# Regrouping the sparse pairs of a layer: chunks 0 to 4 and 5 to 6 instead of 0 to 3 and 4 to 6, with five buffers for fetched values

## The chip, the cores and the metric

The kernel runs on one core of one Trainium2 chip. The metric is the device time of one execution in microseconds (us); lower is better. Engines are named as in the profile: PE (TensorE, matmuls; PEld is its weight load), DVE (VectorE), ACT (ScalarE), POOL (GpSimd, which also issues the indirect gathers), SP (SyncE, which issues the plain DMAs). A "q" behind a name is that engine's instruction queue.

## The reference

Two layers, each of the form norm, modulation, mixer, gated residual, norm, modulation, experts, gated residual, on x of shape (4, 1024, 256). Cut to layer 1, which is what the change touches:

```python
B, S, H = 4, 1024, 256
h = layernorm(x) * (1 + ca) + sa
x = x + ga * fast_weights(h)              # chunks of 128 tokens, one after the other
h = layernorm(x) * (1 + cb) + sb
x = x + gb * experts(h)

def step(carry, x_chunk):                 # fast_weights: a scan over 8 chunks
    a0, a1, a2, acc = carry
    out = (silu(x_chunk @ a0) * (x_chunk @ a2)) @ a1
    loss = mean((out - x_chunk) ** 2)
    decay = 1.0 - 0.001 * loss
    return (a0 * decay, a1 * decay, a2 * decay, acc + loss), out

def experts(x):                           # E = 8 experts of 256 x 256, top 2 of them
    probs = softmax(x @ router_w.T)
    vals, idx = top_k(probs, 2)
    w = vals / (vals.sum(-1, keepdims=True) + 1e-6)
    return ((x @ W[idx] + probs[idx]) * w).sum(over the two)
```

Layer 0 has a linear attention and 8 experts with a hidden layer of 1024 and top 2; the change does not touch it.

## The kernel before

All values are float32. The token axis is cut into 8 chunks of 128 tokens; one chunk has B = 4 tiles (one for each batch) of 128 tokens by 256 features. x stays on the chip in `x_sb` during the whole kernel.

**The order of the work.** From the start of layer 1 to the end the order of the instructions on PE, ACT, DVE, POOL and SP is set by a planner, the class `Plan`. Each piece of work is given an engine, an estimated duration, the pieces it must come after, the buffers ("slots") it holds and a `rank`. `Plan.run` plays the pieces through in model time: an engine that is free takes, among the pieces that are ready and whose slots are to be had, the one of the lowest rank. The order that comes out is the order in which the instructions stand in each engine's queue, and each queue runs strictly in that order on the chip. Slots are counted in `room1`, and are freed in the order in which they were taken. Ranks count in chunks: most pieces of chunk c have ranks near c.

**Layer 1, chunk by chunk** (the loop `for c in range(NC)` at the end of the kernel):

- `combine("c1", ...)`, for each of the 4 tiles, fetches layer 0's two expert values (one plain DMA on SP into a `yg1` buffer), weighs and adds them to `x_sb`. `normal(("n1", c), ...)` norms and modulates the chunk and transposes it.
- `fast` computes the fast weights: 64 matmuls `p_u` (L1967, 128x512 outputs), the gates on ACT (L1979) and DVE (L1983), 64 matmuls `p_f` (L2015), the difference on DVE (L2037), its square on ACT (L2050), the gated step on DVE (L2056) and its addition to `x_sb` on POOL (L2063). The sum of the squares goes through the matmul `pm_loss` (L2080) to the next chunk's `decay`.
- `normal(("n2", c), ...)` norms the chunk again (`pm_t`, L1620). `routed` computes the router's logits (`pm_l`, L2107), picks two experts for each token and marks them in a group's tables. `shares` turns the logits into weights and biases. The normed rows go to DRAM (`ga_rows`, `gb_rows`; SP).

**Groups of sparse pairs.** A pair is a token with one of its two experts. Chunks 0 to 3 form group `ga` (n = 16 tiles), chunks 4 to 6 group `gb` (n = 12); the class `Pairs` holds a group's tables. When a group's last chunk has been routed, `closed` counts the pairs of each expert (`turn`, `turned`, `total`, `close`, `across`, `limits`) and ranks them (`bases`, `ranks`, `places`, `slots`). The pairs are then worked off in J = 2n + 7 blocks of 128 pairs of one expert each: 39 for `ga` and 31 for `gb`. The tables of up to 16 tiles times 8 experts fit the 128 partitions; a larger group has them in `halves`.

One block is the function `block`: `reach` on DVE (L724, once for each half), the count matmul `look` on PE (L737, once for each half), `find` on DVE (L750 and L759), a gather of 128 rows on POOL (L332, `xg`), two transposes on PE (L2259, `pm_x`), a copy on ACT (L2265), four matmuls with the expert's weights (L2276, `p_e`; two in the program, four in the trace), a copy on ACT (L2286) and a plain store to `ga_y` or `gb_y` on SP (L2289).

When all blocks of a group are stored, `combine("c2", ...)` brings the values back: for each tile two gathers on POOL (L332, `yg`) into a `yg2` buffer of which there are three, a weighing on ACT (L1504) and three steps on DVE (L1510, L1513, L1515), the last of them the addition to `x_sb`. After 4 tiles the finished chunk is stored to the output on SP (L2464).

**Chunk 7** is not sparse: `dense` multiplies it with all 8 experts (64 matmuls of 128x512, L2324) and sums with weights on DVE (L2340, L2349), then L2369 and L2370 and a store for each batch (L2373).

Ranks that matter here: blocks of `ga` run from 4.57 to 6.07 (base 4.57, span 1.5), of `gb` from 7.35 to 8.01; the combinations have 6.49 and 7.89, each plus 0.2 for each further chunk; the second norm of chunk 7 has 7.65; the dense experts have 8.23 plus 0.1 for each batch. Within a block, `reach`, the count and `find` stand 0.4 ahead of the block's own rank.

Of the kernel before, what the change touches and what calls it, by code (L numbers as in the profile page):

```python
# [19 lines left out]
P = 128  # L20
B, S, D = 4, 1024, 256
NC = S // P
KD = D // P
E = 8
# [6 lines left out]
SPARE = 3  # L31
FIRST = 8
ROUTER = 64
AHEAD = 3
DX = D + 2
W1ROW = KD * H + KH
# [102 lines left out]
def adaln_d2_kernel(  # L139
# [29 lines left out]
    ps_m = ctx.enter_context(tc.tile_pool(name="ps_m", bufs=3, space=PSUM))  # L169
# [72 lines left out]
    rank = const.tile([P, E], F32, name="rank")  # L242
# [7 lines left out]
    for dst, sign, op in ((upto16, 1, ALU.is_ge), (past16, -1, ALU.is_gt)):  # L250
# [5 lines left out]
            base=0,  # L256
# [87 lines left out]
    class Pairs:  # L344
# [4 lines left out]
        def __init__(self, pool, scratch, name, n):  # L349
            def t(shape, dt, what, of=pool):  # L350
                return of.tile(shape, dt, name=f"{name}_{what}", bufs=1)

            self.n, self.J, self.name = n, blocks_of(n), name

            self.part = min(n, P // E)
            self.halves = n // self.part
            self.K = self.part * E
            self.one = t([P, 2, n, E], F16, "one")
            self.best = t([P, 2, n], F32, "best")
            self.w = t([P, 2, n], F32, "w")  # L360
            self.pos = t([P, 2, n], F32, "pos")
            self.slot = t([P, 2, n], I32, "slot")

            self.meta = t([P, n, 2], F32, "meta")
            nc.vector.tensor_copy(self.meta[:, :, 1], twice[:, :n])
            self.beyond = t([P, 2], F32, "beyond")
            nc.vector.memset(self.beyond, float(2 * n * P))
            self.code = t([P, self.J], F32, "code")
            self.row = t([P, self.J], I32, "row")
            self.wrow = t([P, self.J], I32, "wrow")  # L370
            self.start = t([P, E], F32, "start")


            self.more = t([P, self.halves, P + 1], F16, "more")
            nc.vector.memset(self.more[:, :, P : P + 1], 1.0)
            self.limit = t([P, self.halves, self.J], F32, "limit")
            self.nth = t([P, self.J], F32, "nth")

            self.both = t([P, n + 1, E], F16, "both")
            nc.vector.memset(self.both[:, 0, :], 0.0)  # L380
            self.pairs = t([P, self.halves, P], F16, "pairs")
            self.base = t([P, self.halves], F32, "base", scratch)
# [63 lines left out]
        def turned(self, pt, h):  # L446
            nc.scalar.copy(self.pairs[: self.K, h, :], pt[:, 1, :])
            nc.scalar.copy(self.more[: self.K, h, :P], pt[:, 0, :])
# [950 lines left out]
    with tc.manual_schedule(engines=ORDERED):  # L1399
# [8 lines left out]
    ew = l1.tile([P, E, KD, D], F32, name="ew")  # L1408
    SHA, SCA, GA, SHB, SCB, GB = range(6)
    mods1 = [l1.tile([P, B, D], F32, name=f"mod{i}") for i in range(6)]  # L1410
    groups = [Pairs(l1, l1, "ga", 4 * B), Pairs(l1, l1, "gb", 3 * B)]
    mod_rows1 = dram.tile([B, 6, D], F32, name="mod_rows1")
    early = ctx.enter_context(tc.tile_pool(name="early", bufs=1))
    poolF = tc.tile_pool(name="poolF", bufs=2, side="right")
# [7 lines left out]
        p2=2,  # L1422
        pm=3,
        yg1=3,
        yg2=3,
        h1=2,
        h2=2,
        hT1=2,
# [753 lines left out]
    def closed(g, after, rank):  # L2182

        key = g.name
        ps = plan.slot("pm")

        def turn():
            made[key, "turn"] = g.turn(ps_m, 0)

        def bases():  # L2190
            made[key, "bases"] = g.bases(ps_m)

        def ranks():
            made[key, "ranks"] = g.ranks(ps_m)

        m = plan(PE, 0.3, turn, after=after, holds=[ps], rank=rank)
        t = plan(
            ACT, 0.7, lambda: g.turned(made[key, "turn"], 0), after=[m], holds=[ps], rank=rank
        )
        ps = plan.slot("pm")  # L2200
        m = plan(PE, 0.15, lambda: g.total(ps_m), after=[t], holds=[ps], rank=rank)
        d = plan(DVE, 2.3, lambda: g.close(late), after=[m], holds=[ps], rank=rank)
        ps = plan.slot("pm")
        m = plan(PE, 0.15, bases, after=[t], holds=[ps], rank=rank)
        b = plan(
            ACT, 0.2, lambda: g.based(made[key, "bases"]), after=[m], holds=[ps], rank=rank
        )
        ps = plan.slot("pm")
        m = plan(PE, 0.4, lambda: g.across(ps_m), after=[d], holds=[ps], rank=rank)
        e = plan(DVE, 0.2, g.list_experts, after=[m], holds=[ps], rank=rank)  # L2210
        d = plan(DVE, 1.1, lambda: g.limits(late), after=[e, b], holds=[ps], rank=rank)
        ps = plan.slot("pm")
        m = plan(PE, 0.3, ranks, after=[t], holds=[ps], rank=rank + 0.3)
        s = plan(
            DVE,
            0.8,
            lambda: g.places(late, made[key, "ranks"]),
            after=[m],
            holds=[ps],
            rank=rank + 0.3,  # L2220
        )
        s = plan(DVE, 0.8, lambda: g.slots(late), after=[d, s], rank=rank + 0.5)
        return d, e, s

    def block(g, j, rows, y, lists, experts, stored, rank):
# [7 lines left out]
        def count_():  # L2233
            made[key, "counts"] = g.look(ps_m, made[key, "reached"])

        hit = plan.slot("reached")
        r = plan(DVE, 0.28, reach, after=[lists], holds=[hit], rank=rank - 0.4)
        m = plan(PE, 0.15, count_, after=[r], holds=[look, hit], rank=rank - 0.4)
        f = plan(
            DVE,  # L2240
            0.6,
            lambda: g.find(late, made[key, "counts"], j),
            after=[m],
            holds=[look],
            rank=rank - 0.4,
        )
        xg, ps, xTs = plan.slot("xg"), plan.slot("pm"), plan.slot("xT")

# [47 lines left out]
    def dense(c, slotT, ts, d, x, rank):  # L2296
# [19 lines left out]
        for b in range(B):  # L2316
            last, st = [], plan.slot("step")
            for j in range(E // 2):
                ps = plan.slot("p1")

                def mm(b=b, j=j):
                    p1 = made[key, b, j] = psum(ps_1, [P, 2, D], "p1_e")
                    for k in range(KD):
                        nc.tensor.matmul(  # L2324
                            p1,
                            lhsT=made["n2", c, "hT"][:, k, b, :],
                            rhs=ew[:, 2 * j : 2 * j + 2, k, :],
                            start=(k == 0),
                            stop=(k == KD - 1),
                        )  # L2330

                def out_(b=b, j=j):
                    if j == 0:
                        made[key, "sum", b] = tiny([P, D], "step")
                    w, sum_ = made[key, "w"], made[key, "sum", b]
                    for i in range(2):
                        e = 2 * j + i
                        p = made[key, b, j][:, i, :]
                        if e == 0:
                            nc.vector.tensor_scalar(  # L2340
                                sum_,
                                p,
                                w[:, b, e : e + 1],
                                vb[:, b : b + 1],
                                ALU.mult,
                                ALU.add,
                            )
                        else:
                            nc.vector.scalar_tensor_tensor(  # L2349
                                sum_, p, w[:, b, e : e + 1], sum_, ALU.mult, ALU.add  # L2350
                            )

                m = plan(
                    PE, 1.74, mm, after=ts, holds=[ps, slotT], rank=rank + 0.1 * b + 0.02 * j
                )
                last = [
                    plan(
                        DVE,
                        0.95,
                        out_,  # L2360
                        after=[m, x, *last],
                        holds=[ps, st],
                        rank=rank + 0.1 * b + 0.02 * j - 0.5,
                    )
                ]

# [8 lines left out]
            f = plan(DVE, 0.9, done, after=last, holds=[st], rank=rank + 0.1 * b)  # L2375
            plan(SP, 0.1, store, after=[f], rank=rank)

    last_pairs = Pairs(l1, l1, "gc", B)
    lasts = {"decay": [], 0: [], 1: []}
    y_of = [dram.tile([g.J * P, D], F32, name=f"{g.name}_y") for g in groups]  # L2380
    rows_of = [dram.tile([g.n * P + 1, D], F32, name=f"{g.name}_rows") for g in groups]
    vbs = [l1.tile([P, g.n], F32, name=f"{g.name}_vb") for g in groups]
    stored = {0: [], 1: []}
    for g, rows in zip(groups, rows_of):
        for k in range(KD):
            nc.sync.dma_start(rows[g.n * P :, k * P : (k + 1) * P], ones[:1, :])
    for c in range(NC):
# [3 lines left out]
        else:  # L2391
# [16 lines left out]
        sums, decay = fast(c, slot, slotT, ts, lasts["decay"])  # L2408
        lasts["decay"] = decay
        slot, slotT, hs, ts = normal(  # L2410
            ("n2", c), c, "2", [[d] for d in sums], (SHB, SCB), 7.65 if c == NC - 1 else c + 0.92, [range(B)]
        )
        which = 0 if c < 4 else 1
        if c == NC - 1:
            d, x = routed(last_pairs, c, 0, slotT, ts, 7.46)
            dense(c, slotT, ts, d, x, 8.23)
            continue
        g, first = groups[which], 4 * which
        at = (c - first) * B
        d, x = routed(g, c, at, slotT, ts, c + 1.05)  # L2420
        shares(g, c, at, vbs[which], x, c + 1.5)
# [8 lines left out]
        stored[which].append(  # L2430
            plan(SP, 0.1, store, after=hs, holds=[slot], rank=c + 1.1, lag=3.5)
        )
        if c in (3, 6):
            lists, experts, slots = closed(g, lasts[which], c + 0.97)
            base, span = ([4.57, 1.5], [7.35, 0.66])[which]
            ys = [
                block(
                    g,
# [10 lines left out]
            for q in range(first, c + 1):  # L2449
# [7 lines left out]
                    vbs[which],  # L2457
                    mods1[GB],
                    [*ys, slots],
                    (6.49, 7.89)[which] + 0.2 * (q - first),  # L2460
                )

                def store(q=q):
# [2 lines left out]
                        x_sb[:, q, :, :],  # L2466
                    )

                plan(SP, 0.1, store, after=done, rank=(6.4, 8.2)[which] + 0.2 * (q - first))
    with tc.manual_schedule(engines=ORDERED | {EngineType.SP}):  # L2470
        plan.run()

# [56 lines left out]
```

## Time and profile before

| | |
|---|---|
| median of 3 runs | 1135.76 us (1135.41 to 1138.16) |
| profiled execution | 1146.41 us |
| its span, first to last instruction | 1144.4 us |
| mean granted TensorE clock | 0.988 |
| PE busy | 1096.9 us (96%) |
| DVE busy | 590.8 us (52%) |
| ACT busy | 425.5 us (37%) |
| POOL busy | 422.0 us (37%) |
| layer 1's first p_u matmul | at 629 us |
| group ga: last chunk's router, first fetch of a block, first gather of a combination | at 829.6, 843.4, 963.2 us |
| group gb: last chunk's router, first fetch of a block, first gather of a combination | at 1018.8, 1033.4, 1100.0 us |
| last matmul ends | at 1131.3 us |

The profile is of one execution; its time is longer than the median of the runs, and its parts are compared with its own span. A line of a group gives the line of the kernel, the engine, the operation, output and input, the number of instructions, their busy time in us and the mean duration of one in ns, and behind the second bar the idle time of the engine just ahead of them with what ended it. A line of a timeline gives the start, the length, the engine, the line and operation, and in brackets the idle time before it. A line of stretches gives the stretch, its length, the busy time and number of instructions of PE, PEld, DVE, ACT and POOL, the granted clock, the share of DMA time and GB/s.

### The profile page before, as it was taken

The numbers are of one execution on the slowest core, as the hardware profiler recorded it, in microseconds if no ns is written. First come the engines' busy times: TensorE is split into PE (matmuls) and PEld (weight loads), VectorE is DVE, ScalarE is ACT, GpSimd is POOL, SyncE is SP. The second block draws the span as 40 slices with busy tenths as digits, with TensorE's granted clock in tenths as the row PEclk, the third lists the DMA queues.
The fourth block names the chain that finished last, engine by engine and source line by source line (L and its number), as shares of the span: only waits on it lengthen the run. The fifth ranks groups of instructions, "written<-read, shape, count | busy, mean of one in ns | idle before, by whom it ended". The sixth has DMA issues, their size and how long they took to land.

```text
span 1144.4 us, 18476 instructions
## 1 busy us (share of the span) xinstructions
PE 1096.9 (96%) x6231; PEld 870.8 (76%) x6231; DVE 590.8 (52%) x2305; ACT 425.5 (37%) x1148; POOL 422.0 (37%) x483
## 2 busy tenths in 40 slices
PE   8999999999999999999999999999999999899893
PEld 5996899999999999999988466566666676656741
DVE  7777332222222222222265688866777535787566
ACT  5975233333322333332243342422425225242521
POOL 1000455555555555555553010010034332635643
PEclk8999999999999999999999999999999999999997
DMA  9424449442332415142161212100014223333543
GB/s 316 156 56 94 149 144 315 139 137 92 114 115 66 158 39 176 51 154 75 55 229 39 84 46 74 47 10 19 18 41 133 82 69 102 106 107 97 139 112 123
DMA packets 77693, 122.38 MB, mean 107 GB/s; under 512 B 27341, under 2 KB 57302, under 8 KB 72991
## 3 DMA queue, kind: packets, MB, share of 16 engines
q0 software_dynamic: 31872, 69.68, 19.7%
q1 hardware_dynamic: 44622, 49.92, 13.9%
q10 hardware_dynamic: 1104, 1.58, 0.4%
q8 instruction: 52, 0.85, 0.3%
q14 instruction: 43, 0.34, 0.1%
HBM read 205.25 MB, written 30.22 MB: 206 GB/s over the span
## 4 chain that ended last, share of the span: by engine, by line
PE 82%; DVE 7%; DMA 4%; issue 3%; ACT 2%; POOL 1%; ACTq 0%; POOLq 0%; SPq 0%; DVEq 0%
PE p_h L1658 20%; PE p_y L1681 19%; PE p_u L1967 17%; PE p_f L2015 8%; PE p_e L2276 4%; PE p_e L2324 2%; PE pm_x L2259 1%; PE pm_l L2107 1%; DMA w<-in_W,g_wrow 1%; PE pm_x L1638 1%; PE pm_counts L737 1%; PE pm_gram L1100 1%; PE pm_t L1620 1%; PE pm_b L1041 1%; PE pm_l L1233 1%
## 5 line engine op out<-in xcount | busy, mean ns | idle before, releaser
L1670 ACT ACTIVATE hid<-p_h,w 128x128 f32<-128x128 f32 x544 | 154.8, 368 | 324.7 <-issue 256.4
L1658 PEld LDWEIGHTS p_h<-xT,w 128*128 128x128 f32 x2176 | 253.1, 192 | 5.7 <-DVE xT L1643 1.6
L1658 PE MATMUL p_h<-xT,w 128*128 128x128 f32 x2176 | 254.4, 275 | 1.8 <-DVE xT L1643 1.2
L1681 PE MATMUL p_y<-w,hid 128*128 128x256 f32 x1088 | 249.0, 382 | 0.3 <-issue 0.3
L1967 PE MATMUL p_u<-hT,a 128*128 128x512 f32 x512 | 232.6, 599 | 1.7 <-ACT hf L1979 0.9
L1681 PEld LDWEIGHTS p_y<-w,hid 128*128 128x128 f32 x1088 | 201.6, 190 | 25.2 <-issue 0.5
L1967 PEld LDWEIGHTS p_u<-hT,a 128*128 128x128 f32 x512 | 94.8, 191 | 99.3 <-issue 90.4
L332 POOL DMA_INDIRECT w<-in_W,g_wrow x134 | 135.0, 1007 | 77.3 <-ACT hid L1670 47.0
L1643 DVE COPY xT<-pm_x 128x256 f32<-128x256 f32 x68 | 28.8, 424 | 186.8 <-PE pm_x L1638 143.4
L784 POOL DMA_INDIRECT y<-y,g_dest x68 | 69.5, 1022 | 143.7 <-DVE g_reached L724 108.4
L2015 PE MATMUL p_f<-a,hf 128*128 128x256 f32 x512 | 116.3, 380 | 0.8 <-ACT y L2286 0.8
L1692 DVE TENSOR_TENSOR y<-p_y,w 128x256 f32<-128x256 f32 x68 | 28.9, 425 | 167.1 <-PE p_y L1681 160.8
L332 POOL DMA_INDIRECT xg<-h_rows,g_row x68 | 66.7, 980 | 124.6 <-DVE g_hits L750 104.2
L2015 PEld LDWEIGHTS p_f<-a,hf 128*128 128x128 f32 x512 | 96.1, 190 | 18.8 <-issue 5.7
L2063 POOL TENSOR_TENSOR x_sb<-x_sb,step 128x256 f32<-128x256 f32 x32 | 24.4, 763 | 175.1 <-DVE step L2056 122.1
L332 POOL DMA_INDIRECT xg<-ga_rows,ga_row x39 | 37.3, 956 | 91.3 <-DVE ga_row L759 35.0
L2276 PE MATMUL p_e<-ew,xT 128*128 x280 | 70.4, 384 | 0.3 <-ACT y L2286 0.3
L1979 ACT ACTIVATE hf<-p_u,decay 128x512 f32<-128x512 f32 x56 | 38.2, 685 | 83.2 <-PE p_u L1967 73.6
L2276 PEld LDWEIGHTS p_e<-ew,xT 128*128 128x128 f32 x280 | 49.5, 190 | 10.3 <-issue 4.7
L1578 DVE TENSOR_TENSOR h<-h,mod 128x256 f32<-128x256 f32 x128 | 51.5, 426 | 7.0 <-ACT h L1568 3.9
L1983 DVE SCALAR_TENSOR_TENSOR hf<-p_u,decay,hf 128x512 f32<-128x512 f32 x56 | 41.9, 748 | 23.0 <-PE p_u L1967 16.3
L2286 ACT COPY y<-p_e 128x256 f32<-128x256 f32 x70 | 25.9, 371 | 56.0 <-PE p_e L2276 26.6
(362 smaller groups left out, 1291.6 us busy)
## 6 DMA issues: line engine op xcount, KB each, us to landing
yg<-y SPq DMA_DIRECT2D x32, 256.0 KB
ga_y<-y SPq DMA_DIRECT2D x39, 128.0 KB
x_sb<-in_x SPq DMA_DIRECT2D x8, 512.0 KB
h_rows<-xn SPq DMA_DIRECT2D x8, 512.0 KB
gb_y<-y SPq DMA_DIRECT2D x31, 128.0 KB
out_x<-x_sb SPq DMA_DIRECT2D x7, 512.0 KB
a<-in_fw SPq DMA_DIRECT2D x6, 512.0 KB
mod<-mod_rows SPq DMA_DIRECT2D x6, 512.0 KB
```

The lines of the kernel that those rows point to most:

```text
L332: return nc.gpsimd.indirect_dma_start(out=dst, out_offset=None, in_=table, in_offset=bass.IndirectOffsetOnAxis(ap=index, axis=0), bounds_c ...
L784: nc.gpsimd.indirect_dma_start(out=table, out_offset=bass.IndirectOffsetOnAxis(ap=dest, axis=0), in_=y, in_offset=None, bounds_check=2 * s ...
L1578: nc.vector.tensor_tensor(h, h, mods1[(sc, sh)[i]][:, b, :], (ALU.mult, ALU.add)[i])
L1658: nc.tensor.matmul(p1[:, i, :], lhsT=w1[:, k * H + m * P : k * H + (m + 1) * P], rhs=xT[:, k, :], start=(k == 0), stop=(k == KD - 1),)
L1670: nc.scalar.activation(hid[:, m, :], p1[:, i, :], AF.Relu, bias=w1buf[j % 2][:, KD * H + m : KD * H + m + 1],)
L1681: nc.tensor.matmul(p2, lhsT=hid[:, m, :], rhs=w2[:, m * D : (m + 1) * D], start=(m == 0), stop=(m == KH - 1),)
L1692: nc.vector.tensor_tensor(y, p2, w2buf[j % 2][:, KH * D :], ALU.add)
L1967: nc.tensor.matmul(pu, lhsT=a[:, k, m * P : (m + 1) * P], rhs=made["n1", c, "hT"][:, k, :, :], start=(k == 0), stop=(k == KD - 1),)
L1979: nc.scalar.activation(made[key, m], made[key, m, 0], AF.Silu, scale=decays[c])
L1983: nc.vector.scalar_tensor_tensor(h, made[key, m, 1], decays[c], h, ALU.mult, ALU.mult)
L2015: nc.tensor.matmul(made[key, "p2", b], lhsT=made[key, m][:, b * P : (b + 1) * P], rhs=a1[:, m, :], start=(m == 0), stop=(m == KH - 1),)
L2276: nc.tensor.matmul(made[key, "p2"], lhsT=made[key, "xT"][:, k, :], rhs=ew_flat[:, bass.ds(made[key, "at"] + k * D, D)], start=(k == 0), st ...
```

## The change

Layer 1's groups are now described by a table. The first one takes chunks 0 to 4 (n = 20, 47 blocks, two halves of 10 tiles), the second chunks 5 and 6 (n = 8, 23 blocks, one half). `closed` turns and copies each half. The `yg2` buffers are five instead of three. The ranks of the second norm of chunk 7, of the blocks, of `reach`, the count and `find` within a block, of the dense sums on DVE, of the combinations and of the output stores are set anew.

```diff
+GROUPS = ((0, 5), (5, 7))
...
-            self.part = min(n, P // E)
-            self.halves = n // self.part
+            self.halves = -(-n // (P // E))
+            self.part = n // self.halves
...
-    groups = [Pairs(l1, l1, "ga", 4 * B), Pairs(l1, l1, "gb", 3 * B)]
+    groups = [
+        Pairs(l1, l1, f"g{'abc'[i]}", (end - first) * B) for i, (first, end) in enumerate(GROUPS)
+    ]
...
-        yg2=3,
+        yg2=5,
...
     def closed(g, after, rank):
...
-        m = plan(PE, 0.3, turn, after=after, holds=[ps], rank=rank)
-        t = plan(
-            ACT, 0.7, lambda: g.turned(made[key, "turn"], 0), after=[m], holds=[ps], rank=rank
-        )
+        t = []
+        for h in range(g.halves):
+            if h:
+                ps = plan.slot("pm")
+            def turn(h=h):
+                made[key, "turn", h] = g.turn(ps_m, h)
+            def turned(h=h):
+                g.turned(made[key, "turn", h], h)
+            m = plan(PE, 0.3, turn, after=after, holds=[ps], rank=rank)
+            t.append(plan(ACT, 0.7, turned, after=[m], holds=[ps], rank=rank))
...
     def block(g, j, rows, y, lists, experts, stored, rank):
...
-        r = plan(DVE, 0.28, reach, after=[lists], holds=[hit], rank=rank - 0.4)
-        m = plan(PE, 0.15, count_, after=[r], holds=[look, hit], rank=rank - 0.4)
+        r = plan(DVE, 0.28, reach, after=[lists], holds=[hit], rank=rank - 0.2)
+        m = plan(PE, 0.15, count_, after=[r], holds=[look, hit], rank=rank - 0.2)
         f = plan(
             DVE,
             0.6,
             lambda: g.find(late, made[key, "counts"], j),
...
-            rank=rank - 0.4,
+            rank=rank - 0.2,
...
     def dense(c, slotT, ts, d, x, rank):
...
                         out_,
                         after=[m, x, *last],
                         holds=[ps, st],
-                        rank=rank + 0.1 * b + 0.02 * j - 0.5,
+                        rank=rank + 0.1 * b + 0.02 * j - 0.28,
...
-            ("n2", c), c, "2", [[d] for d in sums], (SHB, SCB), 7.65 if c == NC - 1 else c + 0.92, [range(B)]
+            ("n2", c), c, "2", [[d] for d in sums], (SHB, SCB), 7.5 if c == NC - 1 else c + 0.92, [range(B)]
...
-        which = 0 if c < 4 else 1
+        which = next((i for i, (_, end) in enumerate(GROUPS) if c < end), None)
...
-        g, first = groups[which], 4 * which
+        g, first = groups[which], GROUPS[which][0]
...
-        if c in (3, 6):
+        if c + 1 == GROUPS[which][1]:
             lists, experts, slots = closed(g, lasts[which], c + 0.97)
-            base, span = ([4.57, 1.5], [7.35, 0.66])[which]
+            base, span = ((5.45, 0.6), (7.4, 0.5))[which]
...
-                    (6.49, 7.89)[which] + 0.2 * (q - first),
+                    (6.3, 7.79)[which] + 0.2 * (q - first),
...
-                plan(SP, 0.1, store, after=done, rank=(6.4, 8.2)[which] + 0.2 * (q - first))
+                plan(SP, 0.1, store, after=done, rank=(6.3, 7.79)[which] + 0.2 * (q - first))
```

Left out of the diff: two tables of pieces by group that now have as many entries as `GROUPS`, the lists of copies that `closed` hands on, and the name of chunk 7's tables (`gd`, was `gc`).

## The prediction

> **What bounds the kernel now.** I read the page first: the chain that ended last, then the 40 slices, then the busy time by stage, then the timeline of single engines.
>
> ```profile
> PE 82%; DVE 7%; DMA 4%; issue 3%; ACT 2%; POOL 1%; ACTq 0%; POOLq 0%; SPq 0%; DVEq 0%
> ...
> PE   8999999999999999999999999999999999899893
> ...
> PEclk8999999999999999999999999999999999999997
> ```
>
> The chain is PE, and PE is idle almost only in the last two slices. Any change must remove PE work, PE idle time, or what follows PE's last matmul. The stages I cut at the events of the timeline (columns: stretch, its length, busy time of PE, its weight loads, DVE, ACT, POOL):
>
> ```profile
> 640.00:740.00 100.00, 100.00 (x348) 60.33 (x347) 88.02 (x282) 38.48 (x81) 6.68 (x8) 1.00 0.21 64
> ...
> 843.40:959.90 116.50, 112.75 (x513) 80.14 (x512) 68.74 (x290) 46.46 (x126) 43.14 (x47) 1.00 0.31 91
> ...
> 1033.40:1062.20 28.80, 26.02 (x138) 20.33 (x137) 21.12 (x106) 8.70 (x27) 17.34 (x19) 1.00 0.38 110
> 1062.20:1097.00 34.80, 30.73 (x166) 23.71 (x164) 18.74 (x92) 16.96 (x49) 15.13 (x16) 1.00 0.53 141
> 1097.00:1131.40 34.40, 28.47 (x61) 11.31 (x59) 25.11 (x58) 6.38 (x11) 19.62 (x21) 0.95 0.34 103
> 1131.40:1144.40 13.00, 0.00 (x0) 0.00 (x0) 7.53 (x18) 1.20 (x2) 3.78 (x4) 0.62 0.44 142
> ```
>
> Row 1 is chunks 0 to 2 without blocks: no PE idle at all. Row 2 holds the 39 blocks of group a: 3.75 us idle. Rows 3 and 4 hold the 31 of group b: 2.78 + 4.07 = 6.85 us. The last block ends at 1097.0; from there to the end are 47.4 us (rows 5 and 6): the dense experts of chunk 7 and the 12 combinations of chunks 4 to 6. Their groups, in that stretch:
>
> ```profile
> L2324 PE MATMUL p_e<-ew,hT 128*128 128x512 f32 x60 | 28.5, 627 | 5.9 <-DVE step L2349 5.9
> ...
> L332 POOL DMA_INDIRECT yg<-gb_y,gb_slot x24 | 23.4, 975 | 25.4 <-DMA gb_y<-y 12.6 <-DVE x_sb L1515 6.7 <-issue 4.9
> ```
>
> POOL issues 24 gathers, start to start 1.25 us (0.95 and 0.30 of issue), and waits 6.7 us for a yg buffer to come free. First gather 1099.98, last 1135.22, end 1144.4. The sum 2.9 + 23 x 1.25 + 6.7 + 9.2 = 47.6 us is the tail: POOL's gathers set the end, and PE has finished 13 us before it. One more stall is in PE's timeline, in chunk 6:
>
> ```profile
> 967.63 10.52 PE L1967 MATMUL p_u<-hT,a 128*128 128x512 f32 x24
> ...
> 1000.41 0.39 PE L2080 MATMUL pm_loss<-loss,ones 128*128 128x4 f32 x2 [3.29 <-ACT diff L2050]
> 1000.65 13.96 PE L1967 MATMUL p_u<-hT,a 128*128 128x512 f32 x28
> ```
>
> ACT's square for the loss stood behind a combination (L1504) whose gather, issued at 993.42, took 3.91 us; POOL had stood 2.56 us before it for a buffer. PE lost 3.29 us, and then 28 matmuls took 13.96 us where 24 had taken 10.52 (28 would take 12.27): 1.7 us of lower clock (granted 0.88 from 1000.6 to 1014.6).
>
> **The change part by part.** Blocks: 2n + 7 with n = 16 and 12 gives 39 + 31 = 70; with 20 and 8 gives 47 + 23 = 70. No expert matmul is added or removed. n = 20 passes the 16 that fit 128 partitions, so group a now has two halves of 10.
>
> *Second half, on PE.* Each of 47 blocks has a second count matmul (L737), and one more reach (L724).
>
> ```profile
> 1031.82 0.33 PE L737 MATMUL pm_counts<-gb_more,g_reached 96*128 96x129 f16 x3
> ...
> 1043.29 0.28 PE L737 MATMUL pm_counts<-gb_more,g_reached 96*128 96x129 f16 x2
> ...
> 310.82 0.41 DVE L724 TENSOR_SCALAR g_reached<-count,g_limit 128x128 f16<-128x128 f16 x2
> ...
> 862.57 0.24 DVE L724 TENSOR_SCALAR g_reached<-count,ga_limit 128x128 f16<-128x128 f16 x1
> ...
> 865.36 0.95 DVE L724 TENSOR_SCALAR g_reached<-count,ga_limit 128x128 f16<-128x128 f16 x1
> ```
>
> A further count costs 0.33 - 0.28, some 0.055 us: 47 x 0.055 = 2.6 us. Closing the group adds 9 small matmuls (3 turn, 1 total, 2 bases, 3 ranks): 0.5. PE is full there, so **+3.1 us**; 0 if all fall into the 3.75 us of idle time, 5.5 if each pays its 98 ns weight load (56 x 0.098). The second copy pair of `turned` on ACT (0.26 + 0.28 us) lengthens the 13.8 us from chunk 3's router (829.6) to the first fetch (843.4) by some 0.5 us; chunk 5's 64 p_u matmuls (27.5 us) hide it, and without them it costs those 0.5.
>
> *Eight blocks move ahead of chunk 6.* One is 0.22 (two transposes) + 0.86 (four p_e) + 0.06 of PE: 9.1 us leave a full stretch and enter a full one: 0. Their DVE, ACT, POOL and SP steps go with them (8 x 1.25 us of fetches on POOL). What changes is idle PE time per block: 3.75/39 = 0.10 in group a, 6.85/31 = 0.22 in group b. Group a's ranks become denser (47 over 0.6 of a chunk; were 39 over 1.5), like b's 31 over 0.66, but chunk 6's p_u (rank from 6.0) are there to fill: I take 0.15, and keep 0.22 for b. 47 x 0.15 + 23 x 0.22 - 10.6 = **+1.5** (-3.7 with 0.10 for all, +4.8 with 0.22).
>
> *Five yg2 buffers.* Removes waits for `x_sb L1515`: 11.9 us on POOL in group a's combinations (963 to 1021), 6.7 in the tail. For chunk 6's stall of 3.29 + 1.7 = 5.0 us I take half: the gather is issued earlier, but now 20 combinations come, and 20 at the old pace (16 in 57 us) need 71 us, where POOL had 86 us between the last fetch of group a (947) and the first of b (1033), 16 of them waiting for stores. With five buffers the pace can fall to 2.5 us each. Queued behind a waiting gather on POOL are the four x_sb adds (L2063) that chunk 6's second norm needs; behind a waiting L1504 on ACT, the squares. **-2.5** (-5.0 to +5.0, a second such stall). On SP one more 512 KB output store moves out of the tail; it waits for its combinations, with group b's row store behind it, which in before was issued at 1013.99, straight after its source.
>
> *The tail.* 16 gathers instead of 24. From the last block: by POOL 2.9 + 15 x 1.25 + 9.2 = 30.9 us without a wait. By PE: 60 matmuls x 0.43 (44 took 19.05) = 25.8, then DVE 1.9 and 4.7 from the last store to the end: 32.4. By DVE: 25.11 + 7.53 busy, less four combinations of 1.32 = 27.4; with 1.8 to the first product and 4.7: 33.9. So when POOL is relieved DVE is late next, and the ceiling is 47.4 - 33.9 = 13.5 us. Not all comes: PE waited 5.9 us in four places for DVE, and the x4 at 1127.71 took 3.63 us for the 1.88 of its kind. Half of those 7.6 us kept gives 37.7: **-9.7** (-13.5 to -3.4, if the waits grow to a tail of 44). That is also 8 x 1.25 = 10.0 with every wait as it was.
>
> *Cover for chunk 7's norm and router.* From its last p_f (1062.2) to its weights (1090.96) are 28.8 us, filled by 22 blocks. With 23 in all, perhaps 14 remain: 14 x 1.14, 3.5 of transposes and router, and three PSUM banks of dense work at 1.72 = 24.7 us. **+1.5** (0, since the chain is also freed of blocks and its rank falls from 7.65 to 7.5; 4.1 if not). The other ranks (-0.4 to -0.2, -0.5 to -0.28) add no instruction: they let the combinations (7.79) go ahead of the dense sums on DVE; that is in the tail's range.
>
> *Sum:* 3.1 + 1.5 - 2.5 - 9.7 + 1.5 = **-6.1 us**. The profiled execution took 1146.41 us (1144.4 span and 2.0 around it), 0.9% over the median of 1135.76; I carry the microseconds over: **1129.7 us**.
>
> *Two rules weighed.* A reach has a median of 247 ns and a mean of 325 in group a; the one of 0.95 us above ended with POOL's add (865.50, 0.75 us). So 47 more cost DVE some 47 x (0.17 + 0.08) = 12 us, and gathers (956 ns with blocks and without) are not slowed. The Trainium skill, "SBUF — State Buffer", its part on the shared port pair, says that VectorE in a two-port mode and GpSimd exclude each other for a whole instruction; an estimate by that page, each second reach behind a gather, is 47 x 0.95 = 45 us of DVE and would make the change slower. The rows show it for few reaches, and I follow them.
>
> Lower clock: in the tail matmuls at half speed came after single waits of no more than 2.45 us. The Trainium skill, "TensorE: Matmul & The Clock Gate", part 1, puts the drop after an idle window of about 3.4 us; by it, a tail with such short waits would run at full clock and gain 0.9 us more. The row decides.
>
> **The rivals.** *The tail gives it back (25%).* If PE and DVE wait for each other more as combinations go ahead of the sums, POOL's relief is lost: tail 44, gain 3.4, sum +0.2: 1136.0 us. For it: DVE waited 8.7 us before L2349 and PE 5.9 for it, none of it POOL's. Against: two of those waits fell in POOL's 4.9 us wait, which five buffers remove.
>
> *DVE bounds group a's blocks (20%), slower.* Per block DVE has 0.33 + 0.35 + 0.08 + 0.16 + 0.25 = 1.17 us, and 33 us of other work in 116.5 (68.7 less 39 x 0.91), 0.28 per us. The plan still has 0.28 us for a reach. If the blocks are packed to POOL's pace, 59 us, DVE has 47 x 1.17 + 0.28 x 59 = 71.5: 12.5 us too much, and the gates of p_u stand in the same queue. Sum -6.1 + 12.5 = +6.4: 1142.2 us. It decides where a block comes sooner than each 1.17/0.72 = 1.6 us. Against: row 1, where DVE does 88 of 100 us and PE never waits.
>
> **How the numbers follow.** My forecast has 55%: 1129.7, its own range 1123 to 1134. Low end: a full tail gain and no stall in chunk 6, 1135.8 - 6.1 - 3.8 - 2.5 = 1123.4, and 3 us for fewer gaps: 1120. High end: the DVE case, 1142 to 1143. About 0.3% (3.4 us) is what a measurement of this kernel can tell from no change. Under 1132.4: 0.93 of the forecast and 0.15 of the first rival, 0.55. Above 1139.2: 0.85 of the DVE case and a quarter of the first rival, 0.23, with the forecast's edge 0.25. The rest, 0.20, is within.
>
> **What would show it.** Right: 47 + 23 blocks; 16 gathers in the tail, no wait of POOL on L1515 over 2 us; last block to end 34 to 41 us; L737 117 matmuls for layer 1; no PE wait on `diff` over 2 us. Wrong: a tail over 44 us; over 8 us of PE idle time among group a's blocks, before reaches or hits; a second loss stall; PE idle before the dense matmuls over 4 us.

## The result, and the profile after

The changed kernel took 1138.55 us, median of 20 runs (1136.39 to 1141.54); the kernel before, in 20 runs beside it, 1135.93 us (1133.30 to 1139.29). The ratio is 1.0023, 95% interval [1.0014, 1.0031]: some 2.6 us slower, just inside what I had called no change, where I had forecast 6.1 us less.

The profiled execution of the changed kernel took 1141.54 us, its span is 1139.2 us, and against the first profile of the kernel before (1144.4) that looks like the forecast: 5.2 us less. It is not. Later I got a profile of the kernel before (run e13, span 1132.4) on a chip where it takes 1135.4 us, as in the 20 runs. Those two make the comparison here, each counted from the first router matmul of layer 1 (690.1 and 693.6), because that point shifts by up to 3.5 us between the profiles of one program. (The profiled execution of the changed kernel is the slowest of its 20 runs, so the whole spans are not compared.)

Stretches of e13, the kernel before: the stages from router to router, then to the last block, to PE's last matmul, to the end (columns as in the prediction):

```profile
690.10:825.30 135.20, 135.20 (x488) 84.21 (x487) 102.16 (x349) 45.59 (x97) 9.22 (x12) 1.00 0.10 30
825.30:886.20 60.90, 57.56 (x271) 40.20 (x270) 44.31 (x200) 22.86 (x62) 23.12 (x25) 1.00 0.28 85
886.20:963.30 77.10, 75.90 (x327) 52.19 (x326) 37.36 (x147) 28.81 (x76) 22.11 (x25) 1.00 0.28 83
963.30:1013.60 50.30, 47.82 (x160) 28.49 (x158) 38.17 (x113) 18.64 (x37) 29.13 (x32) 0.97 0.35 106
...
1089.80:1117.80 28.00, 25.96 (x60) 10.98 (x59) 23.56 (x55) 5.78 (x10) 19.33 (x20) 1.00 0.40 120
1117.80:1132.40 14.60, 0.00 (x0) 0.00 (x0) 8.87 (x22) 1.80 (x3) 4.18 (x5) 0.61 0.44 138
sum 442.30, PE 414.80 PEld 269.57 DVE 307.20 ACT 153.99 POOL 142.07; mean PE 51.85 PEld 33.70 DVE 38.40 ACT 19.25 POOL 17.76
```

The same of the changed kernel:

```profile
693.60:873.70 180.10, 180.10 (x649) 111.89 (x648) 127.84 (x437) 58.98 (x126) 12.14 (x16) 1.00 0.08 25
873.70:976.30 102.60, 94.43 (x521) 72.53 (x520) 66.36 (x335) 42.98 (x123) 48.12 (x51) 0.98 0.43 124
976.30:1032.50 56.20, 56.20 (x183) 32.40 (x182) 43.92 (x124) 23.36 (x45) 39.98 (x43) 1.00 0.43 128
...
1103.20:1132.20 29.00, 26.23 (x61) 10.81 (x59) 25.27 (x62) 5.17 (x9) 16.45 (x16) 1.00 0.34 105
1132.20:1139.20 7.00, 0.00 (x0) 0.00 (x0) 3.52 (x9) 0.00 (x0) 0.00 (x0) 0.68 0.34 114
sum 445.60, PE 423.07 PEld 273.84 DVE 314.72 ACT 155.18 POOL 143.41; mean PE 60.44 PEld 39.12 DVE 44.96 ACT 22.17 POOL 20.49
```

The sums differ by 3.3 us, the medians by 2.6. In it: the tail (last two rows) 42.6 to 36.0, **-6.6**; PE busy before the tail 388.84 to 396.84, **+8.0**; PE idle before the tail 10.86 to 12.76, **+1.9**. Chunk 6's stall is gone, as the row of 56.20 of 56.20 us shows. The timeline of PE in chunk 6, first e13, then the changed kernel:

```profile
992.61 1.88 PE L1967 MATMUL p_u<-hT,a 128*128 128x512 f32 x4
996.97 0.39 PE L2080 MATMUL pm_loss<-loss,ones 128*128 128x4 f32 x2 [2.48 <-ACT diff L2050]
997.21 13.96 PE L1967 MATMUL p_u<-hT,a 128*128 128x512 f32 x28
```

```profile
1015.94 1.88 PE L1970 MATMUL p_u<-hT,a 128*128 128x512 f32 x4
1017.66 0.31 PE L2083 MATMUL pm_loss<-loss,ones 128*128 128x4 f32 x2
1017.83 12.26 PE L1970 MATMUL p_u<-hT,a 128*128 128x512 f32 x28
```

The wait of 2.48 us and the half clock behind it (13.96 us for 28 matmuls against 12.26) are both gone from chunk 6: 4.2 us. The half clock has only moved: the changed kernel has a window of it, as long, at 970.8 us, among the blocks of `ga`. The tail by its groups, e13 and then the changed kernel:

```profile
L2324 PE MATMUL p_e<-ew,hT 128*128 128x512 f32 x60 | 26.2, 594 | 2.0 <-DVE step L2349 2.0
L332 POOL DMA_INDIRECT yg<-gb_y,gb_slot x24 | 23.5, 979 | 20.6 <-DMA gb_y<-y 12.4 <-issue 4.3 <-DVE x_sb L1515 1.4
```

```profile
L2333 PE MATMUL p_e<-ew,hT 128*128 128x512 f32 x60 | 26.4, 594 | 2.7 <-DVE step L2358 2.7
L333 POOL DMA_INDIRECT yg<-gb_y,gb_slot x16 | 16.5, 1028 | 13.6 <-DMA gb_y<-y 9.0 <-issue 4.0 <-DVE yg L1513 0.3
```

Here is the first thing that the first profile did not show: in e13 POOL waits 1.4 us for a buffer in the tail, where the first profile had 6.7, and PE 2.0 us for DVE where that had 5.9. The prediction's own formula gives e13's tail, that of the kernel before: 2.9 + 23 x 1.25 + 1.4 + 9.2 = 42.3 us (measured 42.6). And the groups of the blocks' matmuls from 690 us on, e13 and the changed kernel:

```profile
L2276 PE MATMUL p_e<-ew,xT 128*128 x280 | 70.3, 384 | 0.3 <-ACT y L2286 0.3
L737 PE MATMUL pm_counts<-ga_more,g_reached 128*128 128x129 f16 x39 | 7.8, 221 | 0.0
```

```profile
L2285 PE MATMUL p_e<-ew,xT 128*128 x280 | 73.4, 394 | 1.3 <-ACT y L2295 1.3
L738 PE MATMUL pm_counts<-ga_more,g_reached 80*128 80x129 f16 x94 | 10.5, 222 | 0.2 <-DVE ga_row L760 0.2
```

The second thing: the same 280 expert matmuls take 3.1 us more. Matmuls overlap, so I also counted each from its start to the next one's start (or its own end): p_e 224 to 238 ns (280, +3.8 us), pm_x 125 to 136 ns (140, +1.6), the transposes of the norms pm_t +0.4, the counts 6.3 to 9.0 us (+2.7), the groups' lists +0.8, p_u -1.8 (the half clock), p_f +0.5: the +8.0.

The third thing is the shape of the counts. The first number of `64*128` in a line of PE is the rows of the matmul: the tiles of a half times 8 experts. It was 128 (`ga`) and 96 (`gb`); now it is 80 and 64. Two places in the changed kernel, one in `ga` and one in `gb`, each a count (or two) with the four p_e behind it:

```profile
960.22 0.28 PE L738 MATMUL pm_counts<-ga_more,g_reached 80*128 80x129 f16 x2
960.34 1.08 PE L2285 MATMUL p_e<-ew,xT 128*128 x4
...
1075.96 0.23 PE L738 MATMUL pm_counts<-gb_more,g_reached 64*128 64x129 f16 x1
1076.12 1.13 PE L2285 MATMUL p_e<-ew,xT 128*128 x4
```

Two counts of 80 rows hold PE for 0.12 us, one of 64 rows for 0.16. Over the whole trace a count ahead of another matmul takes 57 ns with 128 rows and a median of 60 with 96 or 80, but a mean of 152 with 64 (14 of them). The first p_e behind it takes 271, 269, 274 and, with 64 rows, 320 ns, where a p_e behind a p_e takes 222 to 226. The 14 places with 64 rows thus cost 14 x (0.09 + 0.05) = 2.0 of the +8.0 us.

### The profile page after: what moved, and what is told of

Its sections match the earlier page's. It is cut to its first block, busy times and chain, and to the rows that moved or that the text cites. A ratio compares the mean times of both kernels' runs of the same rounds, so it can differ in the third digit from the quotient of the medians.

```text
span 1139.2 us, 18653 instructions
## 1 busy us (share of the span) xinstructions
PE 1102.1 (97%) x6287; PEld 875.8 (77%) x6287; DVE 596.6 (52%) x2352; ACT 427.5 (38%) x1150; POOL 424.4 (37%) x483
## 5 line engine op out<-in xcount | busy, mean ns | idle before, releaser
L1970 PE MATMUL p_u<-hT,a 128*128 128x512 f32 x512 | 228.5, 595 | 1.5 <-ACTq L1933 0.9
L2285 PE MATMUL p_e<-ew,xT 128*128 x280 | 73.4, 394 | 1.3 <-ACT y L2295 1.3
L1982 ACT ACTIVATE hf<-p_u,decay 128x512 f32<-128x512 f32 x56 | 38.4, 685 | 86.4 <-PE p_u L1970 84.4
L333 POOL DMA_INDIRECT xg<-ga_rows,ga_row x47 | 45.2, 961 | 64.0 <-DVE ga_row L760 47.7
L333 POOL DMA_INDIRECT yg<-ga_y,ga_slot x40 | 38.8, 970 | 24.0 <-DMA ga_y<-y 12.6
```

The costliest lines, as they stand in the source:

```text
L333: return nc.gpsimd.indirect_dma_start(out=dst, out_offset=None, in_=table, in_offset=bass.IndirectOffsetOnAxis(ap=index, axis=0), bounds_c ...
L1970: nc.tensor.matmul(pu, lhsT=a[:, k, m * P : (m + 1) * P], rhs=made["n1", c, "hT"][:, k, :, :], start=(k == 0), stop=(k == KD - 1),)
L1982: nc.scalar.activation(made[key, m], made[key, m, 0], AF.Silu, scale=decays[c])
L2285: nc.tensor.matmul(made[key, "p2"], lhsT=made[key, "xT"][:, k, :], rhs=ew_flat[:, bass.ds(made[key, "at"] + k * D, D)], start=(k == 0), st ...
```

## The experiments

The chips differ, and not in speed alone. Layer 0 and the first chunks of layer 1 take the same everywhere (in all 20 profiles the first router matmul of layer 1 starts at 688.5 to 693.6 us, and a chunk without blocks takes 45.0 us); but on five of the six chips that my runs got, the kernel before takes 1143 to 1146 us and the changed one, on the three of them where it ran, 1.8 to 1.9% more; on the sixth (e11 to e13) the kernel before takes 1136 us as in the 20 runs. Ratios are to the kernel before on the same chip.

**e1, the kernel before again**, and **e6**, the same on another chip (e7 on a third).

> The unchanged kernel before, profiled a second time. Theory A (the profiled execution on which the prediction was built was not a typical one: its wait of 3.29 us before pm_loss in chunk 6 with 1.7 us of lower clock, and the half-speed matmuls and waits in the tail, are matters of chance): this execution takes 1134 to 1138 us, PE does not wait over 1 us before chunk 6's pm_loss, and from the last block to the end are at most 43 us instead of 47.4. Theory B (the profile shows what every execution does, and the missing gain is somewhere in the changed kernel): the wait before pm_loss is there again with 3 us or more, and the tail is 46 to 48 us.

> The kernel before, profiled a third time. Theory A: if before takes about 1136 us here, its profile shows no wait over 1 us before chunk 6's pm_loss and a tail of 38 to 42 us from the last block to the end; if it takes about 1146 us, the wait of 3.5 us and the tail of 47 us are there as in the two earlier profiles. Theory B: the wait and the tail of 47 us are there whatever the time.

Measured: 1146.97 us, ratio 1.0006 [0.9989, 1.0023]; 1144.15 us, 0.9998 [0.9986, 1.0011]; e7 1144.93 us, 1.0013 [1.0001, 1.0025]. All have the wait of 3.3 to 3.5 us before `pm_loss` and a tail of 47.0 to 47.2 us, as the first profile had: it shows a kernel of 1144 us, not of 1136.

**e2, five buffers alone** (also e14 and e18).

```diff
-        yg2=3,
+        yg2=5,
```

> The kernel before with five yg2 buffers instead of three, nothing else. Theory A (the waits for yg buffers rarely reach PE): within 0.2% of before, 1134 to 1138 us. Theory B (they cost 2.5 to 5 us in chunk 6 and some in the tail in every execution): 0.3 to 0.8% faster, 1127 to 1132 us. If the model time of the planner, which takes a gather to land in 1.5 us, puts more weighings on ACT ahead of data that has not landed: slower by up to 0.3%.

Measured: 1152.16 us, ratio 1.0052 [1.0035, 1.0069]; e14 1147.88 us, 1.0041 [1.0021, 1.0060]; e18 1148.03 us, 1.0040 [1.0020, 1.0059]. The wait before `pm_loss` goes, but PE now waits for ACT's and DVE's `hf`, and the tail grows to 51.6 to 53.2 us. ACT and DVE in turn stand still for something new (from e2: line, waited for, total, times, longest; "remote" is a signal that no instruction ending at that time explains):

```profile
DVE step L2349 <- remote: 10.0, 2, 5.4
...
DVE hf L1983 <- remote: 6.4, 1, 6.4
...
ACT hf L1979 <- remote: 4.0, 1, 4.0
```

**e3, two halves alone**: the code after, with the groups, ranks and buffers of before, and the 16 tiles of `ga` listed in two halves of 8 (also e15).

```diff
-GROUPS = ((0, 5), (5, 7))
+GROUPS = ((0, 4), (4, 7))
-            self.halves = -(-n // (P // E))
+            self.halves = 2 if n == 4 * B else -(-n // (P // E))
```

> The kernel before with its groups and ranks, but group a's 16 tiles in two halves of 8: 39 blocks with a second count matmul and a second reach, and a second turn. The cost of the halves alone: 39 x 0.055 + 0.5 = 2.6 us (0.23%) if PE takes all of it; 0 to 1 if idle time of PE takes it in; 6 us and more if DVE's second reach holds PE up.

> The kernel before, with the lists of its first group worked out in two halves of 8 tiles in place of one of 16: 39 more pm_counts matmul pairs. By my prediction's term (0.055 us for each block) 39 x 0.055 + 0.5 = 2.6 us, ratio 1.002. If the halves also make the blocks' own matmuls dearer (224 to 238 ns each over 280 of them, 3.9 us), 6 us or more, ratio 1.005 or more, and p_e's mean in this run is over 230 ns.

Measured: 1154.45 us, ratio 1.0069 [1.0048, 1.0089]; e15 1150.32 us, 1.0056 [1.0037, 1.0076]. Six to eight us for 39 further counts, where my term gives 2.6. In e15 the counts of `ga` alone go from 3.4 (e14, same chip) to 8.2 us. But a half of 8 tiles has 64 rows, where the change's halves of 10 tiles have 80: in e15 a count of 64 rows ahead of another matmul takes 150 ns (32 places), and a p_e behind it 320. That is some 32 x (0.09 + 0.05) = 4.5 us which the halves of the change do not pay, so e3 and e15 do not price them. Nor do they show the halves to make p_e much dearer: its mean is 233 ns in e15 against 226 in e14, but seven of e15's fall in a window at half clock, and the others take 228, as in e3 (225 in e1 and e2, outside such windows).

**e4, the change with three buffers** (also e16), **e5, the change again** (also e8, e17).

> The changed kernel with three yg2 buffers as before. Theory A (buffers matter little): 1137 to 1141 us. Theory B (five buffers are what lets 20 combinations pass within chunk 6): 3 to 8 us slower than the changed kernel, 1141 to 1147 us, with POOL waiting for DVE's additions and a wait before pm_loss in chunk 6.

> The changed kernel, unchanged, beside the kernel before on one and the same chip, with a second profile. Theory A (the two profiles were taken on chips of different pace, and what the change removes, the wait before pm_loss and the waits in the tail, is there only on a chip where gathers land late): on a chip where before takes 1145 us or more the change is 4 to 7 us faster, on a chip where before takes 1136 us it is 1 to 4 us slower. Theory B (the changed kernel's own costs exceed what it saves on every chip): 1.001 to 1.004 of before on either.

> The changed kernel with three buffers in place of five: groups and ranks alone. On a chip where PE's signals come in time: a wait of 2 to 5 us of PE in chunk 6 comes back, the tail stays at 36 us; ratio to the kernel before 1.004 to 1.007 by the theory that the buffers are worth 2 to 5 us; 1.002 as the changed kernel itself by the rival that they are worth nothing there. On a chip where they come late 1.005 to 1.009 as in its first run.

Measured: e4 1154.14 us, ratio 1.0067 [1.0044, 1.0089]; e16 1151.39 us, 1.0078 [1.0045, 1.0111]; e5 1165.90 us, 1.0190 [1.0169, 1.0210]; e8 1164.38 us, 1.0187 [1.0156, 1.0219]; e17, on e16's chip, 1164.39 us, 1.0183 [1.0155, 1.0212]. Neither theory of e5 allowed for that. On e16's chip the two further buffers cost 13.0 us. The tail is 36 us in e4, e5, e16 and e17: it needs three buffers, not five. Chunk 6 of e5, first ACT, then PE, then POOL:

```profile
1001.84 0.59 ACT L1507 ACTIVATE yg<-yg,ga_vb,ga_w 128x256 f32<-128x256 f32 x1
1014.58 0.69 ACT L1982 ACTIVATE hf<-p_u,decay 128x512 f32<-128x512 f32 x1 [12.15 <-remote]
...
1004.14 1.89 PE L2018 MATMUL p_f<-a,hf 128*128 128x256 f32 x8
1008.47 1.98 PE L1970 MATMUL p_u<-hT,a 128*128 128x512 f32 x4 [2.44 <-DVE hf L1986]
1015.32 3.78 PE L1970 MATMUL p_u<-hT,a 128*128 128x512 f32 x4 [4.87 <-ACT hf L1982]
...
1011.64 0.95 POOL L333 DMA_INDIRECT yg<-ga_y,ga_slot  x1 [0.30 <-issue]
1018.42 0.95 POOL L333 DMA_INDIRECT yg<-ga_y,ga_slot  x1 [5.83 <-DVE x_sb L1518]
```

ACT's gate waits for PE's semaphore alone. The four matmuls it needs end at 1002.59 in the record, and it starts at 1014.58, 20 ns after an update of that semaphore that no matmul's end stands beside. POOL had started 22 gathers from 985.02 to 1011.64, one every 1.25 us; the last late signals came 2.0 to 3.5 us after the last of them had ended. Signals later than 1.8 us stand in the profile of every run on the five chips but e9, each time while POOL issues such gathers one after the other, and in none on the sixth.

**e9, two buffers, and the landing of a gather modelled at 3.0 us; e10, the landing alone** (e8 is the changed kernel beside them).

```diff
-        yg2=5,
+        yg2=2,        # e9 only
-                            lag=1.5,
+                            lag=3.0 if kind == "yg2" else 1.5,
```

> The changed kernel with two buffers for the fetched values in place of five, and the planner told that a gather lands 3.0 us after its issue in place of 1.5, so that ACT and DVE take up the combinations later. A combination then holds its buffer for about 2.5 (two issues) + 2.9 (landing) + 1.4 (DVE) = 6.8 us, and POOL pauses about 0.9 us after every two gathers: no run of gathers is longer than 2. Theory 1 (late signals after a long run of gathers): waits of ACT and DVE that nothing on the core ends, 12.2 + 13.1 + 6.0 us in the changed kernel, fall under 2 us in chunks 6 and 7, and the kernel comes at or below the time of the one before, ratio 0.990 to 1.000. Rival (the stop is ACT and DVE waiting in order for landings): two buffers make it worse, 1.02 or more.

> The changed kernel with five buffers, and only the planner's landing time of a gather of values set from 1.5 to 3.0 us, so ACT and DVE have each combination later in their order while POOL's gathers run on without a pause as before. Theory 1 (late signals after a long run of gathers): the waits that nothing on the core ends stay, 10 us or more in chunk 6, and the ratio stays within 0.005 of the changed kernel's on this chip. Rival (ACT and DVE wait in order for landings that the planner has too early): those waits go, and the kernel is 10 us or more faster than the changed one.

Measured: e9 1159.87 us, ratio 1.0151 [1.0134, 1.0168]; e10 1159.40 us, 1.0129 [1.0102, 1.0155]. In e9 POOL never issues more than five gathers in a row at that pace, and no wait of ACT or DVE over 1 us is left that nothing explains; chunk 6 and the end:

```profile
979.70:1037.60 57.90, 57.90 (x187) 33.25 (x187) 41.74 (x115) 20.60 (x41) 28.71 (x31) 1.00 0.31 95
...
1140.90:1157.20 16.30, 0.00 (x1) 0.00 (x0) 7.85 (x19) 1.81 (x4) 4.73 (x5) 0.62 0.41 130
```

So half of the theory held: without the long runs the signals come in time. The time followed by little: the profile's span is 6.4 us shorter than e8's (1157.2 and 1163.6), the median 4.5. Chunk 6 takes 13.1 us less; from chunk 7's router to the last block are 5.8 us more, and the tail is no shorter (38.6 and 38.4), as the combinations now end 16.3 us after PE. And one loss on these chips is not one of late signals: the stage with `ga`'s blocks takes 107.7 to 109.7 us in all seven profiles of the change's groups there (e9: 109.5), where the first profile of the changed kernel has 102.6 and e11, on the sixth chip, 101.9. In e10 the unexplained waits fall from 28.1 us on ACT's and DVE's `hf` (e8) to 15.9, between what the two theories said.

**e11, two buffers for `ga` and three for `gb`; e12, `ga`'s blocks spread over rank 1.4 in place of 0.6; e13, the kernel before**, all on the sixth chip.

```diff
-        yg2=5,
+        yg2=2, yg3=3,                                   # e11; lag 3.0 for yg2
-            base, span = ((5.45, 0.6), (7.4, 0.5))[which]
+            base, span = ((5.45, 1.4), (7.4, 0.5))[which]   # e12; yg2=3, lag 3.0,
-                    (6.3, 7.79)[which] + 0.2 * (q - first),
+                    (6.9, 7.79)[which] + 0.2 * (q - first),
```

> The changed kernel with two buffers for the fetched values of ga (landing in the planner 3.0 us) and three of their own for gb (1.5 us), five in all. Chunk 6 should be as with two buffers for both (58 us, no idle time of PE, no wait that nothing on the core ends), and the tail as in the changed kernel (36 to 38 us after the last block, 5.7 to 7 us after PE's last matmul, where two buffers left 16.3). If the late end was the only loss of the kernel with two buffers, this one takes 9 to 10 us less, 1150 where the one before takes 1143, ratio 1.005; if the late signals were its whole cause of being slower than before, 0.995 or less.

> The changed kernel with its 47 blocks of ga spread over ranks 5.45 to 6.85 in place of 5.45 to 6.05, so that they lie among chunk 6's matmuls as before those of ga among chunk 5's; the combinations from rank 6.9 in place of 6.3, three buffers, a landing of 3.0 us in the planner. Theory 1 (bunched gathers): PE's idle time in the stage that holds ga's blocks falls from 11 to 12 us to under 4, and no wait over 2 us that nothing on the core ends is left before the tail; the kernel takes 0.985 to 1.000 of the one before. Rival (the blocks' chain through POOL, PE, ACT and DVE costs the same wherever it lies, and later combinations end later): idle time over 8 us all the same or moved to chunk 7's stage, ratio 1.01 or more.

> The kernel before, unchanged, profiled on one more chip. Where it takes about 1144, its stages are those of the four profiles so far (PE waits 3.3 us before pm_loss, 47 us from the last block to the end). Where it takes about 1136, the 8 to 10 us less show in these two places by the theory that its first profile was taken in the slower condition, and in every stage alike by the rival of a slower chip.

Measured: e11 1146.52 us, ratio 1.0094 [1.0069, 1.0119]; e12 1149.62 us, 1.0119 [1.0097, 1.0141]; e13 1135.40 us, 0.9993 [0.9978, 1.0007]. Both are slower than the change itself (1.0023). e11 has a tail of 34.2 us, but PE idles 21.7 us up to its last matmul against 15.5. e12 settles the bunching in the rival's favour: the two stages with `ga`'s blocks idle 4.9 + 4.3 us, the changed kernel's 8.2. p_e has the same mean, 238 ns, but ten of them lie in half-clock windows; the others take 230, where the changed kernel's take 234, and only 22 stand first behind a count, where the changed kernel has 34. No signal is late in any of the three, nor in the first profile of the changed kernel.

I found no version that beats both kernels.

## Why the prediction was wrong

The pair of profiles has +3.3 us where I forecast -6.1: 9.4 us apart, 5.8 of them in PE's work, 3.1 in the tail, 0.5 in PE's idle time.

- **"A full stretch to a full one: 0": this step failed, and it is the larger.** The blocks' matmuls cost 5.4 us more (p_e +3.8, pm_x +1.6). Some 1.7 of it is the window at half clock that in e13 fell on p_u. Outside that window a p_e takes 234 ns where it took 224.5, 2.6 us in all. Of these, 0.9 come from places: 34 p_e stand first behind a count where 16 did, and such a one takes some 50 ns more. Another 0.5 come from rows: group `gb` now has 8 tiles, so 64 rows, and 11 of the 34 take 320 ns for it. Behind a transpose a p_e takes 221 and 218 ns, as before. The rest of p_e and the part of pm_x outside the window (some 1.4) are measured and not explained, and why 64 rows cost more no run shows. The rise is not of one trace: outside half-clock windows p_e is at 224.5 to 226.2 ns in all eight profiles of the kernel before, with three or five buffers, and at 230 to 241 in all ten of the changed groups.
- **Carrying the microseconds of one execution over: this step failed too.** The first profile was 10.7 us over the median, and I carried its microseconds over as if none of that lay in what I meant to remove. By e13 much of it does: of 9.4 us between the two profiles behind the first router matmul, 4.8 are the tail's, 0.8 chunk 6's wait, 3.1 idle time from chunk 7's router to the last block. The tail was 47.4 and is 42.6 in the condition of the median: POOL's wait for a buffer 1.4 us, not 6.7. So the tail's -9.7 was -6.6, though I had its new length too long (37.7 forecast, 36.0 measured).
- **Second halves, +3.1:** near in sum, 2.7 for the counts and 0.8 for the lists. A further count of 80 rows takes 60 ns, close to my 55. But 1.3 of the counts' 2.7 us are the 64 rows of `gb`, which I did not have; in return fewer counts stand ahead of a gap, where I counted their whole 222 ns (2, in e13 12). That the sum came out is in part luck.
- **Idle time per block, 0.15 and 0.22:** right as it stands, 7.6/47 = 0.16 and 4.6/23 = 0.20. What I set it against was not: in e13 the blocks before idle 3.75 and 3.4 us, not 10.6, so this term is +5.1 and not +1.5. No cost shows for the cover of chunk 7 (+1.5 forecast). With half the stall I had +1.35 of idle time in all; the measured +1.9 is close by luck.
- **Five buffers, -2.5:** in this pair chunk 6's wait went whole, -2.5; the half clock behind it, of which I had counted half as saved, came back among the blocks. Alone the buffers were never run where signals come in time, so no run shows that they did it.
- **The sum:** PE's work +2.25 forecast (3.1 less half of 1.7), +8.0 measured; idle +1.35, +1.9; tail -9.7, -6.6: -6.1 became +3.3.
- **The signs that I had named for being right** all came: 47 + 23 blocks, 117 counts, 16 gathers in the tail and no wait of POOL for a buffer over 2 us, 36.0 us from the last block to the end, no wait on `diff` over 2 us. The time rose all the same: none of them looked at how long PE is busy.
- **The rivals:** neither. The tail did not give its gain back. DVE does not bound `ga`'s blocks: PE's idle time among them is 7.6 us, just under the 8 I had named, and half of it (3.8) waits for gathered rows.
- **The two rules.** The Trainium skill, "SBUF — State Buffer", its part on the shared port pair, would have made each second reach wait for a gather; the 94 reaches average 290 ns (331 in e13) with 857 at most, so the row was the better guide. The Trainium skill, "TensorE: Matmul & The Clock Gate", part 1, with its idle window of about 3.4 us, agrees with the tails up to PE's last matmul, which ran at a granted 1.00 across waits of 1.1 to 2.0 us, and not with the window at half clock at 970.8, behind waits of 1.08 and 0.68 us in the last 3.1 us; there the measurement decides.

What stays open: why PE's signals come late on some chips. Their traces also hold fewer records of semaphore updates (8,700 to 9,330, as in the first profile of the kernel before with 9,235, where e11 to e13 and the first profile of the changed kernel have 13,720 to 13,770). The recording may share the cause; no run here tells. Each chip was met once, so whether it is the chip or its state at that hour is open as well.

## What to carry to other kernels

Before summing gains from a profile whose time is over the median, ask whether the excess lies in the very waits that the change removes; only the part that the median also pays can be won. Moving blocks from one full stretch of PE to another is not free if it changes what stands between their matmuls, or the shape of the small ones: take the mean from start to start of the same instruction in both settings, apart from windows at half clock. And more buffers are not safely "at worst nothing": here they let POOL issue faster, and on the chips where they were tried apart the kernel was slower for it by 0.4 to 1.1% (e2, e14, e18; e17 against e16).

## What the runs showed of the hardware

- On five of six chips PE's signals reached ACT and DVE 2 to 12 us after the recorded ends of its matmuls while POOL issued gathers in long runs; in the one run with none over five (e9) not at all, and on the sixth chip not even behind 20 in a row (e13).
- The gathers' data were not late there: from issue to the last packet a median of 2.4 us on either kind of chip.
- One program took 1135.4 us on one chip and 1143 to 1147 on five others, with layer 0 alike.
- A count matmul of 64 rows took 152 ns ahead of a matmul of 128 rows, one of 80, 96 or 128 rows about 60; the first p_e behind it took 320 ns and 269 to 274 (the changed kernel and e13).
